# A two-layer graph attention network on one core: x moves from layer 2's residual product into its first norm, and the second norm's variance to ScalarE

## The chip, the cores and the metric

The kernel runs on one core of one Trainium2 chip. The metric is device time in microseconds from start to end of one execution; lower is better. Engines are named as in the profile: PE (TensorE, matrix products), DVE (VectorE), ACT (ScalarE), POOL (GpSimd) and SP (SyncE, which here only issues DMA transfers). Each engine works through its own instructions in the order of the program and waits where one is not yet free to run.

## The reference

Two graph attention layers (GAT) with residuals over 10,000 nodes and 170,000 edges (80,000 in each direction and 10,000 loops, and the layer adds self loops once more), then a last norm over the sum with the input:

```
def gat_conv(x, edge_index, W, a_src, a_dst, bias, heads, out_ch, concat):
    xl = (x @ W).reshape(n, heads, out_ch)
    e = leaky_relu(alpha_src[src] + alpha_dst[dst], 0.2)
    alpha = softmax of e over the edges of each dst
    out = segment_sum(xl[src] * alpha, dst)
    return out + bias

h0 = x
h = gat_conv(x, edge_index, W1, a_src1, a_dst1, b1, 4, 256, True)
h = relu(layer_norm(h, g1, be1)) + (h0 @ Wr1 + br1)
h1 = h
h = gat_conv(h, edge_index, W2, a_src2, a_dst2, b2, 1, 768, False)
h = layer_norm(h, g2, be2) + (h1 @ Wr2 + br2)
x = _layernorm(x + h)
```

x is 10,000 x 768 in fp32, h1 has 1024 columns, the output is 10,000 x 768. The last norm has no scale and no shift.

## The kernel before, in words

The 10,000 nodes are cut into 79 tiles of 128 (one node per partition). Three stages follow each other.

**Layer 0** (my name for the first loop over tiles, 0 to about 876 us): for each tile the product x W1 with its attention sums goes into a table in DRAM, one row of 1033 numbers a node. Two generators run beside it, one step a tile: `prepare` sorts the nodes by their number of edges and lists each node's neighbours ("slots"), and `weight_steps` loads W2 and Wr1 and folds vectors into them. The PSUM pool of the products has two buffers of 1024 columns.

**Layer 1** (`ordered_layer1`): the tiles are taken by degree, so that all 128 nodes of a tile have about as many neighbours: the numbers of slots n of the 79 steps rise from 8 to 41 (step 39) and fall back to 9, 1377 in all. For each slot POOL issues one indirect DMA (`gather`, L424), which brings one neighbour's table row to each of the 128 partitions. The rows land in a ring of 29 slots, in order; the gather of slot q waits until slot q - 29 is released. Of a tile's n slots the first up to four are summed on PE, by a product with a diagonal matrix of the weights that ACT builds (`summed`, L723 and L729); every fourth of the rest on DVE alone (`weigh`, L519), the others by a multiply on ACT (L508) and an add on DVE (L515). Three slots before a tile's end the logits of the next tile are made (L477 and on), which need all of its rows. At the start of step t the tile before it is normed (L572 to L800). x of the tile, itself gathered by POOL into `xt` (one buffer), is transposed by PE in `from_x` (L699), multiplied by Wr1 (L171), and written by SP to `x_d` (L707), where layer 2 finds it. The next x is gathered after seven slots of the loop and waits for that write. The tile of h1 is transposed, written to `h1_d` (L812) and multiplied by W2 (L817), which gives the rows of layer 2's table. A tile with more slots than the ring goes through `attend_parts`.

**Layer 2** (`ordered_layer2`): the same with a ring of 41 slots and rows of 770 numbers; a tile's own rows come as a plain SP transfer. Of each slot 512 columns are weighed on DVE (L519) and 256 on PE with a diagonal matrix (L927 on ACT, L928 on PE). `residual` puts x and h1 Wr2 into PSUM: x by a product with the identity (L939), then 16 blocks of h1 Wr2 (L942). `norms` runs in steps between the slots of the next tile: statistics of the weighed sum; then (after three slots) scale and shift with g2 and `be2_b`, the add of the residual (L952), and statistics of that sum; then (after six) its mean and deviation in one ACT instruction (L958); then (after nine) POOL's indirect store of the rows (L960). At the start of the layer br1 Wr2 is made by a product of its own (`q`, L965), and br2 and that row are added to `be2_b` after the first tile (L1007, L1008). `fetch_x` loads h1 and x of a tile on SP, two tiles ahead.

All of it stands in the order in which Python emits it; nothing reorders the instructions of an engine.

Of the kernel before, what the change touches and what calls it, by code (L numbers as in the profile page):

```python
# [35 lines left out]
P = 128  # L36
# [43 lines left out]
def gnn_kernel(ctx, tc, x, x_cols, src, dst, src_col, dst_col, W1, a_src1, a_dst1, b1, g1, be1, Wr1, br1,  # L80
# [56 lines left out]
    br1_c = consts.tile([P, K1], F32, name="br1_c")  # L137

# [463 lines left out]
    with tc.tile_pool(name="w1", bufs=1) as w1p, tc.tile_pool(name="l1", bufs=2) as io, \  # L602
# [75 lines left out]
    def ordered_layer1():  # L678
        nc.scalar.add_instruction(mybir.InstLoadActFuncSet(name=nc.get_next_instruction_name(), act_func_set_id=6, engine=nc.scalar.engine))
        with tc.tile_pool(name="b1", bufs=1) as pool, tc.tile_pool(name="small1", bufs=2) as small, \  # L680
# [38 lines left out]
            def summed(acc, diagonals, e, q, lo, hi, m):  # L719

                for k in range(lo, hi):
                    for i in range(H1):
                        nc.scalar.activation(diagonals[:, k * H1 + i, :], ident, AF.Copy,  # L723
                                             scale=e[:, k, i:i + 1])
                for k in range(lo, hi):
                    for i in range(H1):

                        c, d = i * DH1, (i + 1) * DH1
                        nc.tensor.matmul(acc[:, c:d], diagonals[:, k * H1 + i, :], ring.slot(q + k)[:, c:d],  # L729
                                         start=(k == 0 and c % BANK == 0),  # L730
                                         stop=(k == m - 1 and (d % BANK == 0 or d == C1)),
                                         skip_group_check=True)

            def weights_of(t):
# [6 lines left out]
                diagonals = pool.tile([P, ON_PE1 * H1, P], F32, name="diagonals")  # L741
                for lo, hi in ((0, min(m, 2)), (min(m, 2), m)):
                    summed(acc, diagonals, e, FIRST[t], lo, hi, m)
# [24 lines left out]
            for t in range(NT + 1):  # L768
# [66 lines left out]
                if live and not whole:  # L835
# [5 lines left out]
                    def some(q, e):  # L841
                        m = min(ON_PE1, e.shape[1])
                        diagonals = pool.tile([P, ON_PE1 * H1, P], F32, name="diagonals")
                        summed(sums, diagonals, e, q, 0, m, m)
# [23 lines left out]
    def ordered_layer2():  # L868
        nonlocal ps_big
        with tc.tile_pool(name="b2", bufs=1) as pool, tc.tile_pool(name="small2", bufs=2) as small, \  # L870
# [28 lines left out]
            adds = [spread(pool, shift, "out", nc.sync)]  # L899
# [3 lines left out]
            nc.vector.tensor_add(b2_b, b2_b, adds[0][:, :C2])  # L903
            adds.append(spread(pool, br2, "out", nc.sync))
# [27 lines left out]
            def residual(t):  # L932


                hT, xt = ins.pop(t)
                r = ps_big.tile([P, 2 * BANK], F32, name="big")
                for c in range(0, C2, BANK):
                    d = min(C2, c + BANK)
                    nc.tensor.matmul(r[:, c:d], ident, xt[:, c:d], start=True, stop=False,  # L939
                                     skip_group_check=True)  # L940
                    for j in range(K1):
                        nc.tensor.matmul(r[:, c:d], hT[:, j, :], wr2[:, j, c:d], start=False,  # L942
# [4 lines left out]
            def norms(t, h, r, means):  # L947
# [17 lines left out]
            q = product(brT, wr2, C2)  # L965
# [4 lines left out]
            for t in range(NT):  # L970
# [11 lines left out]
                else:  # L982
# [301 lines left out]
```

## Time and profile before

| | |
|---|---|
| median of 10 runs | 5344.74 us (5339.65 to 5348.59) |
| the profiled execution, its own time | 5345.81 us |
| its span, first to last instruction | 5343.9 us |
| mean granted PE clock | 0.946 of full speed |
| busy: PE, weight loads, DVE, ACT, POOL | 89%, 53%, 80%, 52%, 60% |
| moved by DMA | 1591.37 MB, 298 GB/s over the span |
| POOL's gathers (L424, ring) | 2675, 991 ns each |
| DVE, 512 or 256 columns of a slot (L519) | 2530, 624 ns each |
| DVE, 1024 columns of a slot (L515) | 801, 1231 ns each |
| PE, residual of layer 2 (L942) | 2464, 487 ns each |

The page gives each engine's busy time and, for the costliest groups, the idle time just before them and what ended it. Stages differ in what limits them, so the prediction reads the same figures by stretches of the span. A wait "<-issue" is time in which the profile shows nothing that was waited for. Busy times of POOL are rough, and PE's matmuls overlap, so that its share is not one of its peak.

### The profile page before, as it was taken

The numbers are of one execution on the slowest core, as the hardware profiler recorded it, in microseconds if no ns is written. First come the engines' busy times: TensorE is split into PE (matmuls) and PEld (weight loads), VectorE is DVE, ScalarE is ACT, GpSimd is POOL, SyncE is SP. The second block draws the span as 40 slices with busy tenths as digits, with TensorE's granted clock in tenths as the row PEclk, the third lists the DMA queues.
The fourth block names the chain that finished last, engine by engine and source line by source line (L and its number), as shares of the span: only waits on it lengthen the run. The fifth ranks groups of instructions, "written<-read, shape, count | busy, mean of one in ns | idle before, by whom it ended". The sixth has DMA issues, their size and how long they took to land. (4 is left out here: it accounts for less than half of the span.)

```text
span 5343.9 us, 59565 instructions
## 1 busy us (share of the span) xinstructions
PE 4768.3 (89%) x15188; PEld 2857.2 (53%) x15191; DVE 4285.0 (80%) x7729; ACT 2799.3 (52%) x8184; POOL 3231.0 (60%) x3159
## 2 busy tenths in 40 slices
PE   8999996999999986578999999999998866889998
PEld 3444443555555544345555555566666544566665
DVE  5884244899999887688899999589988767889998
ACT  3434343677778776677887777433333222223332
POOL 3446465555666654555666655277777657777774
PEclk9999998999999998789999999999998887999999
DMA  4333625899999997699999999599999989999995
GB/s 156 126 99 86 95 92 197 307 338 348 359 359 362 365 340 276 247 328 345 360 364 365 353 336 333 187 385 374 377 367 348 326 269 322 330 348 370 365 386 220
DMA packets 474306, 1591.37 MB, mean 298 GB/s; under 512 B 118327, under 2 KB 122487, under 8 KB 473958
## 3 DMA queue, kind: packets, MB, share of 16 engines
q0 software_dynamic: 322384, 1286.62, 66.0%
q1 hardware_dynamic: 149520, 297.43, 16.4%
q10 hardware_dynamic: 2054, 3.42, 0.2%
q8 instruction: 128, 2.10, 0.2%
q14 instruction: 220, 1.80, 0.1%
HBM read 1431.80 MB, written 177.29 MB: 301 GB/s over the span
## 5 line engine op out<-in xcount | busy, mean ns | idle before, releaser
L424 POOL DMA_INDIRECT ring<-table,slots x2675 | 2651.5, 991 | 1446.5 <-DVE acc L519 344.4
L519 DVE SCALAR_TENSOR_TENSOR acc<-ring,e,acc 128x512 f32<-128x512 f32 (+1 forms) x2530 | 1578.4, 624 | 127.9 <-PE acc L729 52.4
L508 ACT ACTIVATE ring<-ring,e 128x256 f32<-128x256 f32 x3284 | 1337.4, 508 | 0.0
L515 DVE TENSOR_TENSOR acc<-acc,ring 128x1024 f32<-128x1024 f32 x801 | 985.7, 1231 | 79.6 <-ACT ring L508 10.6
L928 PE MATMUL big<-ring,diagonals 128*128 128x256 f32 x2754 | 682.9, 410 | 201.0 <-ACT diagonals L927 191.2
L171 PE MATMUL big<-w,xT 128*128 128x512 f32 x1896 | 825.5, 597 | 23.3 <-DMA w<-in_W_dram 9.9
L171 PE MATMUL big<-wr,xT 128*128 128x512 f32 x1896 | 833.6, 596 | 0.2 <-ACT xT L700 0.2
L817 PE MATMUL half<-w,hT 128*128 128x512 f32 (+1 forms) x2528 | 830.4, 486 | 0.0
L942 PE MATMUL big<-wr,w 128*128 128x512 f32 (+1 forms) x2464 | 823.0, 487 | 0.0
L928 PEld LDWEIGHTS big<-ring,diagonals 128*128 128x128 f32 x2754 | 561.6, 206 | 319.3 <-ACT diagonals L927 221.1
L817 PEld LDWEIGHTS half<-w,hT 128*128 128x128 f32 x2528 | 477.8, 189 | 372.7 <-issue 310.0
L729 PE MATMUL acc<-ring,diagonals 128*128 128x256 f32 x1912 | 485.7, 412 | 203.9 <-ACT diagonals L723 203.7
L942 PEld LDWEIGHTS big<-wr,w 128*128 128x128 f32 x2464 | 469.6, 191 | 329.8 <-issue 297.9
L171 PEld LDWEIGHTS big<-w,xT 128*128 128x128 f32 x1896 | 362.0, 192 | 482.4 <-issue 464.4
L171 PEld LDWEIGHTS big<-wr,xT 128*128 128x128 f32 x1896 | 357.0, 192 | 420.5 <-issue 419.8
L729 PEld LDWEIGHTS acc<-ring,diagonals 128*128 128x128 f32 x1912 | 392.1, 208 | 289.9 <-ACT diagonals L723 226.9
L576 ACT ACTIVATE sd<-mv,eps 128x1 f32<-128x1 f32 x237 | 69.6, 294 | 813.8 <-DVE mv L574 813.7
L927 ACT ACTIVATE diagonals<-ident,e 128x128 f32<-128x128 f32 x1377 | 411.2, 387 | 141.1 <-DVE e L499 121.3
L723 ACT ACTIVATE diagonals<-ident,e 128x128 f32<-128x128 f32 x956 | 292.8, 387 | 204.3 <-DVE e L499 204.0
L660 DVE TENSOR_TENSOR scr<-big,ad_b 128x1024 f32<-128x1024 f32 x79 | 96.7, 1224 | 376.4 <-ACT row L657 376.4
L485 ACT ACTIVATE e<-e 128x68 f32<-128x68 f32 (+29 forms) x160 | 38.2, 239 | 650.7 <-DVE e L484 650.7
L665 POOL TENSOR_TENSOR row<-row,none 128x1024 f32<-128x1024 f32 x79 | 187.1, 2369 | 261.8 <-ACT row L657 260.7
(172 smaller groups left out, 3618.1 us busy)
## 6 DMA issues: line engine op xcount, KB each, us to landing
ring<-table,slots POOLq DMA_INDIRECT x2675, 6.9
table<-row SPq DMA_DIRECT2D x79, 516.0 KB, 3.5
h_d<-hT SPq DMA_DIRECT2D x79, 512.0 KB, 6.9
w<-h_d SPq DMA_DIRECT2D x77, 512.0 KB, 8.3
table<-row SPq DMA_DIRECT2D x79, 385.0 KB, 6.9
ring<-table SPq DMA_DIRECT2D x79, 385.0 KB, 6.5
xT<-in_x_cols_dram SPq DMA_DIRECT2D x79, 384.0 KB, 4.4
x_d<-xt SPq DMA_DIRECT2D x79, 384.0 KB, 7.2
```

Source lines behind the costliest of these rows:

```text
L171: nc.tensor.matmul(p[:, c:e], aT[:, j, :], w[:, j, c:e], start=(j == 0), stop=(j == k - 1))
L424: nc.gpsimd.indirect_dma_start(out=to, out_offset=None, in_=table, in_offset=bass.IndirectOffsetOnAxis(ap=index, axis=0), **more)
L508: nc.scalar.activation(row[:, s], row[:, s], AF.Copy, scale=e[:, h:h + 1])
L515: nc.vector.tensor_add(acc[:, :c], acc[:, :c], row[:, :c])
L519: nc.vector.scalar_tensor_tensor(acc[:, s], row[:, s], e[:, h:h + 1], (acc if first is None else first)[:, s], op0=OP.mult, op1=OP.add)
L665: nc.gpsimd.tensor_add(row[:, :C1], row[:, :C1], b1_b)
L723: nc.scalar.activation(diagonals[:, k * H1 + i, :], ident, AF.Copy, scale=e[:, k, i:i + 1])
L729: nc.tensor.matmul(acc[:, c:d], diagonals[:, k * H1 + i, :], ring.slot(q + k)[:, c:d], start=(k == 0 and c % BANK == 0), stop=(k == m - 1 ...
L817: nc.tensor.matmul(q, hT[:, j, :], w2[:, j, c:c + q.shape[1]], start=(j == 0), stop=(j == K1 - 1))
L927: nc.scalar.activation(diagonals[:, k % G, :], ident, AF.Copy, scale=e[:, k, :])
L928: nc.tensor.matmul(to, diagonals[:, k % G, :], ring.slot(FIRST[t] + k)[:, ON_PE2:C2], start=False, stop=(k == n - 1), skip_group_check=True)
L942: nc.tensor.matmul(r[:, c:d], hT[:, j, :], wr2[:, j, c:d], start=False, stop=(j == K1 - 1 and (d < C2 or not whole(t))), skip_group_check= ...
```

## The change

- A constant tile `after2` (128 x 768) is made in layer 0: be2 + br2 + br1 Wr2, spread over the partitions. Eight more steps of `weight_steps` each load one block of 128 rows of Wr2 on SP, multiply it by a block of br1 on PE, and add the result to `after2` on DVE.
- In layer 1 POOL adds `after2` to `xt` in place, after the transposes and before SP writes it to `x_d`.
- The diagonal matrices of layer 1 are in three buffers of one slot each in place of one buffer of four slots, and each slot's matrices are built and used in turn.
- In layer 2 `residual` no longer has x in it. x comes into three buffers in turn (one of them `after2`'s, free by then), and stands where `be2_b` stood, as the added vector of the first norm. be2, br2 and the product br1 Wr2 are gone from the start of the layer.
- The add of the residual is one DVE instruction that also sums its rows (`accum_out`). From the sum ACT makes the mean, the variance by a square with an accumulator, the deviation, and the normed rows. The statistics of the second norm on DVE are gone.

```diff
@@ constants
+    after2 = consts.tile([P, C2], F32, name="after2")
@@ weight_steps
             load(w2, W2)
+            nc.sync.dma_start(after2, bass.AP(tensor=be2.tensor, offset=be2.offset, ap=[[0, P], [1, C2]]))
+            part = spread(w1p, br2, "part", nc.sync)
...
             load(wr1, Wr1)
+            nc.vector.tensor_add(after2, after2, part)
+            for k in range(K1):
+                part = w1p.tile([P, C2], F32, name="part")
+                nc.sync.dma_start(part, Wr2[k * P:(k + 1) * P, :])
+                yield
+                q = product(brT[:, k:k + 1, :], part[:, None, :], C2)
+                nc.vector.tensor_add(after2, after2, q[:, :C2])
             yield
@@ layer 1, from_x
                 moves = halves(xT, xt)
+                nc.gpsimd.tensor_add(xt, xt, after2)
                 nc.sync.dma_start(x_d[t], xt)
@@ layer 1, summed
-            def summed(acc, diagonals, e, q, lo, hi, m):
+            def summed(acc, e, q, lo, hi, m):
                 for k in range(lo, hi):
+                    diagonals = pool.tile([P, H1, P], F32, name="diagonals", bufs=3)
                     for i in range(H1):
-                        nc.scalar.activation(diagonals[:, k * H1 + i, :], ident, AF.Copy,
-                                             scale=e[:, k, i:i + 1])
-                for k in range(lo, hi):
+                        nc.scalar.activation(diagonals[:, i, :], ident, AF.Copy, scale=e[:, k, i:i + 1])
                     for i in range(H1):
                         c, d = i * DH1, (i + 1) * DH1
-                        nc.tensor.matmul(acc[:, c:d], diagonals[:, k * H1 + i, :], ring.slot(q + k)[:, c:d],
+                        nc.tensor.matmul(acc[:, c:d], diagonals[:, i, :], ring.slot(q + k)[:, c:d],
@@ layer 2, start
-            brT = at_end(C1).rearrange("p (k n) -> p k n", n=P)
-            nc.vector.tensor_copy(brT, br1_c[:, :, None].to_broadcast([P, K1, P]))
-            firsts = [(at_end(C1), at_end(D0)) for _ in range(min(2, NT))][::-1]
+            firsts = [at_end(C1) for _ in range(min(2, NT))][::-1]
+            xs = [parts[2][:, :D0], parts[3][:, :D0], after2]
             def fetch_x(t):
-                hT, xt = firsts[t] if t < 2 else (parts[t % 2], parts[2 + t % 2][:, :D0])
+                hT = firsts[t] if t < 2 else parts[t % 2]
                 nc.sync.dma_start(hT, h1_d[t])
-                nc.sync.dma_start(xt, x_d[t])
-                return hT.rearrange("p (k n) -> p k n", n=P), xt
+                nc.sync.dma_start(xs[t % 3], x_d[t])
+                return hT.rearrange("p (k n) -> p k n", n=P)
...
-            g2_b, be2_b = (spread(pool, v, n, nc.sync) for v, n in ((g2, "g2"), (be2, "be2")))
-            adds.append(spread(pool, br2, "out", nc.sync))
+            g2_b = spread(pool, g2, "g2", nc.sync)
@@ layer 2, residual
-                    nc.tensor.matmul(r[:, c:d], ident, xt[:, c:d], start=True, stop=False,
-                                     skip_group_check=True)
                     for j in range(K1):
-                        nc.tensor.matmul(r[:, c:d], hT[:, j, :], wr2[:, j, c:d], start=False,
+                        nc.tensor.matmul(r[:, c:d], hT[:, j, :], wr2[:, j, c:d], start=(j == 0),
@@ layer 2, norms
-                scaled(h, means, stats, g2_b, be2_b)
-                nc.vector.tensor_add(h, h, r[:, :C2])
-                mean, inv = deviation(small, pieces(h, C2 // 2))
+                scaled(h, means, stats, g2_b, xs[t % 3])
+                total = small.tile([P, 1], F32, name="all")
+                nc.vector.scalar_tensor_tensor(h, r[:, :C2], 1.0, h, op0=OP.mult, op1=OP.add, accum_out=total)
                 yield
+                o = pool.tile([P, C2], F32, name="out")
                 less = small.tile([P, 1], F32, name="less")
-                nc.vector.scalar_tensor_tensor(less, mean, -1.0, inv, op0=OP.mult, op1=OP.mult)
-                o = pool.tile([P, C2], F32, name="out")
-                nc.scalar.activation(o, h, AF.Identity, bias=less, scale=inv)
+                nc.scalar.activation(less, total, AF.Copy, scale=-1.0 / C2)
+                nc.scalar.activation(o, h, AF.Square, bias=less, accum_out=total)
+                nc.scalar.activation(total, total, AF.Ln, bias=eps, scale=1.0 / C2)
+                nc.scalar.activation(total, total, AF.Exp, scale=-0.5)
+                nc.scalar.activation(less, less, AF.Copy, scale=total)
+                nc.scalar.activation(o, h, AF.Identity, bias=less, scale=total)
@@ layer 2, before and in the loop
-            q = product(brT, wr2, C2)
...
-                    if not t:
-                        nc.vector.tensor_add(be2_b, be2_b, adds[1])
-                        nc.vector.tensor_add(be2_b, be2_b, q[:, :C2])
```

More of the change, by code (lines that the diff above doesn't have):

```diff
@@ L740, in weights_of @@
                 acc = ps_acc.tile([P, 2 * BANK], F32, name="acc")
-                diagonals = pool.tile([P, ON_PE1 * H1, P], F32, name="diagonals")
                 for lo, hi in ((0, min(m, 2)), (min(m, 2), m)):
-                    summed(acc, diagonals, e, FIRST[t], lo, hi, m)
+                    summed(acc, e, FIRST[t], lo, hi, m)
                     yield acc
@@ L842, in some @@
                         m = min(ON_PE1, e.shape[1])
-                        diagonals = pool.tile([P, ON_PE1 * H1, P], F32, name="diagonals")
-                        summed(sums, diagonals, e, q, 0, m, m)
+                        summed(sums, e, q, 0, m, m)
                         return sums, m
@@ L884, in at_end @@
                 return flat[:, rest:rest + n]
-            brT = at_end(C1).rearrange("p (k n) -> p k n", n=P)
-            nc.vector.tensor_copy(brT, br1_c[:, :, None].to_broadcast([P, K1, P]))
-            firsts = [(at_end(C1), at_end(D0)) for _ in range(min(2, NT))][::-1]
+            firsts = [at_end(C1) for _ in range(min(2, NT))][::-1]
+            xs = [parts[2][:, :D0], parts[3][:, :D0], after2]
             def fetch_x(t):
-                hT, xt = firsts[t] if t < 2 else (parts[t % 2], parts[2 + t % 2][:, :D0])
+                hT = firsts[t] if t < 2 else parts[t % 2]
                 nc.sync.dma_start(hT, h1_d[t])
-                nc.sync.dma_start(xt, x_d[t])
-                return hT.rearrange("p (k n) -> p k n", n=P), xt
+                nc.sync.dma_start(xs[t % 3], x_d[t])
+                return hT.rearrange("p (k n) -> p k n", n=P)
             ins = {0: fetch_x(0)}
             ring.fetch(SLOTS[0])
-            adds = [spread(pool, shift, "out", nc.sync)]
+            added = spread(pool, shift, "out", nc.sync)
             b2_b = spread(pool, b2, "b2", nc.sync)
             ins[1] = fetch_x(1)
-            g2_b, be2_b = (spread(pool, v, n, nc.sync) for v, n in ((g2, "g2"), (be2, "be2")))
-            nc.vector.tensor_add(b2_b, b2_b, adds[0][:, :C2])
-            adds.append(spread(pool, br2, "out", nc.sync))
+            g2_b = spread(pool, g2, "g2", nc.sync)
+            nc.vector.tensor_add(b2_b, b2_b, added[:, :C2])
             assert SLOTS[0] <= rest // R2 and NT > 1
@@ L932, in residual @@
             def residual(t):
-                hT, xt = ins.pop(t)
+                hT = ins.pop(t)
                 r = ps_big.tile([P, 2 * BANK], F32, name="big")
```

## The prediction

> **What bounds the kernel now.** I read the busy times by stage first, because the whole-span shares mix three stages. Columns: stretch in us, its length, busy us of PE, PE's weight loads, DVE, ACT and POOL with instruction counts, granted clock, DMA share, GB/s. The cuts are mine: layer 1 runs from 876 to 3443 us, layer 2 after it.
>
> ```profile
> 876.00:1480.00 604.00, 545.14 (x1785) 318.31 (x1786) 519.30 (x871) 415.07 (x1105) 354.61 (x349) 0.96 0.92 339
> 1480.00:1830.00 350.00, 329.43 (x1113) 199.89 (x1113) 316.77 (x508) 279.03 (x754) 224.67 (x218) 0.99 0.98 363
> 1830.00:2510.00 680.00, 502.38 (x1620) 313.89 (x1620) 550.84 (x876) 477.84 (x1280) 385.78 (x382) 0.86 0.85 308
> ...
> 3496.00:4064.00 568.00, 550.00 (x1944) 372.10 (x1944) 517.67 (x1056) 193.85 (x612) 429.74 (x445) 0.97 0.99 373
> 4064.00:4780.00 716.00, 544.54 (x1850) 381.79 (x1850) 532.75 (x1002) 198.44 (x636) 484.12 (x505) 0.85 0.90 319
> 4780.00:5270.00 490.00, 468.97 (x1665) 316.54 (x1664) 455.62 (x925) 165.27 (x523) 371.75 (x384) 0.98 0.99 374
> ```
>
> PE, DVE and the DMA engines all stand above 0.9 outside the middle, so no one share names the bound. The timeline of POOL does, for layer 2 (start, duration, line; idle time before it in brackets):
>
> ```profile
> 3759.33 0.95 POOL L424 DMA_INDIRECT ring<-table,slots  x1 [0.30 <-PE big L942]
> 3760.59 0.95 POOL L424 DMA_INDIRECT ring<-table,slots  x1 [0.30 <-issue]
> 3761.85 1.01 POOL L960 DMA_INDIRECT out_dram<-out,order  x1 [0.31 <-issue]
> 3763.16 0.98 POOL L424 DMA_INDIRECT ring<-table,slots  x1 [0.30 <-issue]
> ```
>
> A gather costs POOL 0.96 + 0.30 us, back to back. From 3496 to 4064 it issues 445 of them, 568/445 = 1.276 us each; from 4780 to 5270 384, again 1.276. POOL never rests in these stretches, whoever is named as releaser: they are POOL's (and at share 0.99 the DMA engines'), and a cheaper DVE or PE leaves them as they are. From 4064 to 4780 505 issues would need 505 x 1.276 = 644 of 716 us: 72 us of slack is all that can be won there.
>
> In layer 1 POOL has slack, but its place in the order matters. First POOL, then PE, where tile 45 (22 slots) begins:
>
> ```profile
> 2426.84 0.99 POOL L424 DMA_INDIRECT ring<-table,slots  x1 [0.75 <-issue]
> 2428.13 1.00 POOL L424 DMA_INDIRECT ring<-table,slots  x1 [0.30 <-PE acc L729]
> 2430.23 1.08 POOL L424 DMA_INDIRECT ring<-table,slots  x1 [1.09 <-PE acc L729]
> 2431.96 0.99 POOL L424 DMA_INDIRECT ring<-table,slots  x1 [0.65 <-PE acc L729]
> 2433.70 0.99 POOL L424 DMA_INDIRECT ring<-table,slots  x1 [0.74 <-PE half L699]
> 2435.80 0.99 POOL L424 DMA_INDIRECT ring<-table,slots  x1 [1.11 <-DVE acc L519]
> ...
> 2440.94 0.97 POOL L424 DMA_INDIRECT xt<-in_x_dram,order  x1 [1.47 <-PE big L171]
> 2442.21 0.99 POOL L424 DMA_INDIRECT ring<-table,slots  x1 [0.30 <-issue]
> ```
>
> ```profile
> 2423.40 10.03 PE L729 MATMUL acc<-ring,diagonals 128*128 128x256 f32 x32 [4.75 <-ACT diagonals L723]
> 2433.26 0.82 PE L699 MATMUL half<-ident,xt 128*128 128x128 f32 x6
> ```
>
> 2426.84 is the last gather of the tile before, 2428.13 to 2433.70 refill slots 0 to 3, freed one by one by PE's diagonals, and PE transposes x only after them.
>
> **Layer 0: +27 us.** Eight weight steps get a K=1-row product (`product` on one row block: two fp32 passes each of 512 and 256 columns), a 384 KB load on SP and a DVE add. On PE 0.87 + 0.43 = 1.3 us (the starts of L939 and of L942 after it, same shapes); on DVE 0.953 (L952), which fits: a tile comes every 10.3 us and DVE has 9.0 in the busiest (two multiplies 2.45, three L239 passes 5.3, their follow-ups 1.3). The product takes the second of two PSUM buffers, so the next tile's product needs the buffer of the tile just finished: ACT's copy (1.0, L657) and two multiplies (2 x 1.22, L660), 3.4 us in which PE now runs on in the other buffer. 8 x 3.4 = 27; bounds 8 x 1.3 = 10 and, with a late load, 35. PE is the bound here (843 of 876 us), so it counts.
>
> **Layer 1: +80 us.** POOL gets one 128x768 add a tile: 187.1/79 = 2.37 us for 1024 columns (L665), so 1.78. Its wait is the larger thing. It stands behind the last gather of the tile before and ahead of slot 0's, and it overwrites `xt`, so it waits for the transposes. In tile 45: add 2434.2 to 2436.0, slot 0 at 2436.3 instead of 2428.1, then 1.3 us each, slot 4 at 2441.5 instead of 2435.8. SP's `x_d` store follows the add and takes 7.2 us, but the x gather has moved as far. I went through POOL's rows of all tiles this way, keeping every release where it is: slot 0 comes 2.3 to 4.3 us late in tiles of up to 15 slots, 5 to 9 in the larger; POOL has caught up to within 2 us at each tile's end, so nothing accumulates by itself.
>
> Who waits for a late gather: the logits of the next tile (L477), three slots before this tile's end. With a ring of 29, the last gather that they need follows the release of slot n(t)+n(t+1)-30. Two stretches of DVE's waits:
>
> ```profile
> DVE e L477 <- DMA ring<-table,slots: 1.3, 3, 0.6
> ...
> DVE e L477 <- DMA ring<-table,slots: 17.0, 5, 4.5
> ```
>
> The first is 1480 to 1830, the second 1760 to 2110 us. By the landings that the trace gives, the last gather is in 6 to 28 us early for n up to 16, 1 to 9 for 17 and 18, and 0 to 2 for 19 and more. So: (a) n up to 16 nothing: PE, 552 of 583 us busy from 2860 to 3443, hides it; 17 and 18, 17 tiles, a delay of 4 to 6 against that slack and DMA engines at 0.98 that lose their queue: 0.5 each, 8. (b) n = 19 to 21, 17 tiles: 3 to 5 late, of which an emptier queue gives back 2 (issue to landing 5.9 us at the median, 3.5 at the fifth percentile): 2 each, 34. (c) n of 22 and more, 11 tiles: 2.2 to 5.4 late, DMA share already 0.83 to 0.92 and landings 3.4 to 4.7 after issue, nothing given back: 3.5 each, 38. Sum 80, and 2 at the first tile, where the x store waits behind 29 gathers. Bounds: 10 (if the queue hides all but 1 us in (c)) and 200 (2.5, 4.5 and 5.5 us, with (a) on 25 tiles). No row has the add beside layer 1's work; I stay below the middle because a queue smooths.
>
> The three diagonal buffers cost nothing: the fourth build waits for the first slot's matmuls, and PE waits for ACT here (4.75 above), not ACT for PE. If PE were late, ACT would stand for one slot's eight passes, 1.8 us, with its multiplies behind it.
>
> The Trainium skill, "SBUF — State Buffer", section "Who interferes with whom", speaks against the add beyond this: a VectorE instruction with two SBUF inputs and a GpSimd one that reads SBUF exclude each other for a whole instruction. L588 (1.28 us, h and be1 both in SBUF) stands near the add; by the rule up to 1.8 x 79 = 142 us more would be DVE's, an estimate; no row of before has such a pair.
>
> **Layer 2: -24 us.** Per tile DVE loses the add (0.953), two statistics (1.02 together), the aggregate (0.209) and L956 (0.153), 2.33, and gets one pass of 0.95 to 1.02 plus an accumulator read (0.08, L239's): -1.25, 99 us in all. PE loses 1.3 a tile, 103 in all. ACT gains a square (1.02 as L958) and two small ones (0.2): 1.4 a tile on an engine at 0.3; no table load is added in the program. In POOL's stretches none of it shows. In 4064 to 4780 DVE waits 73.7 us for gathers in the rising half alone, and the removed work lies after the release that the awaited gather follows (third slot and `turn`) unless n is 23 or more: 8 tiles x 1.25 = 10. At the start the 16-matmul product goes, but DVE waits for gathers (6.67 at 3465): 3. POOL's small rests at n = 14 and below: 5. After the last gather (5275) DVE is the bound: 4.5 tiles x 1.25 = 6. Bounds -5 and -60 (most of the 72, and these). The x load now waits for L588 of three tiles earlier, and x is wanted only in the norm, three tiles after its load: free. If it were late, DVE would stand in L588.
>
> **Sum.** +27 + 82 - 24 = +85 on the profiled execution's 5345.81 (span 5343.9; median of the runs 5344.74, 0.02% off): 5430.
>
> **Rivals.** *Gathers land in time.* The ring and the DMA queue take up POOL's detour. For it: POOL catches up in each tile; against: (c)'s landings with no slack. Then 10 + 10 - 55 = -35, 5310. It decides if the late slot costs under 1 us a tile and the middle of layer 2 gives back most of its 72. *DMA engines starve every tile.* Between the last gather and slot 0 there are now 6 to 10 us against 1.3, more than a landing. For it: share 0.98 in 1480 to 1830; against: 0.92 before that. +35 + 190 - 5, 5565. *Only the largest tiles suffer*, (c) alone with half the price in layer 0: 14 + 40 - 24 = +30, 5375. That the change does not do what it says: the add and the pass stand in the built order, so only that DVE's saving is visible, -99: a part of the first rival.
>
> **Numbers.** Forecast 0.50 (own range 5395 to 5480), only the largest 0.20, starving 0.10, in time 0.20. The runs tell 0.2% (11 us) from nothing. Faster 0.18, same 0.07, slower 0.75; 5320 to 5510 leaves out half of the first rival and most of the starving.
>
> **What would show it.** Right: in 1830 to 2510 POOL's L424 after the new add, DVE's L477 waits up by tens of us, layer 1 longer, layer 2's POOL stretches unchanged at 1.276 us. Wrong: L477's wait unchanged, or issues in layer 2 still back to back but fewer us in 3496 to 4064, or a new wait of DVE on POOL.

## The result and the profile after

The changed kernel takes 5504.03 us (median of 8 runs, 5498.52 to 5513.34) against 5346.24 us for the kernel before (28 runs beside it). The ratio is 1.0298, 95% interval 1.0289 to 1.0307: about 158 us slower. The profiled execution took 5507.73 us, its span 5505.9.

I cut both spans at the DVE instruction that applies a tile's deviation and shift in its norm (L588 before, L589 after), for the first and the last tile of each layer:

| stretch | before, us | after, us | difference | forecast |
|---|---|---|---|---|
| start to layer 1's first norm (layer 0 and one tile) | 926.4 | 977.1 | +50.6 | +29 |
| layer 1, first to last norm | 2493.8 | 2623.0 | +129.1 | +80 |
| to layer 2's first norm | 74.5 | 71.4 | -3.1 | -3 |
| layer 2, first to last norm | 1831.8 | 1817.1 | -14.7 | -21 |
| rest | 17.3 | 17.3 | 0.0 | 0 |

The differences add up to +162, the two spans' own difference. By stretches (columns as in the prediction; the first three lie in layer 1, the others in layer 2):

```profile
927.00:1530.00 603.00, 543.85 (x1783) 317.49 (x1784) 518.46 (x870) 415.20 (x1105) 384.31 (x369) 0.96 0.90 338
1530.00:1900.00 370.00, 327.78 (x1073) 199.73 (x1074) 303.18 (x481) 270.75 (x728) 224.80 (x218) 0.94 0.86 325
1900.00:2660.00 760.00, 517.76 (x1661) 325.30 (x1660) 565.40 (x904) 487.31 (x1307) 422.91 (x407) 0.83 0.76 284
3671.00:4240.00 569.00, 520.71 (x1840) 355.14 (x1839) 484.91 (x975) 231.46 (x724) 431.41 (x447) 0.96 0.99 373
4240.00:4950.00 710.00, 515.55 (x1759) 365.27 (x1758) 505.16 (x935) 231.36 (x724) 482.18 (x506) 0.84 0.91 322
4950.00:5440.00 490.00, 450.82 (x1578) 306.12 (x1577) 431.07 (x866) 197.80 (x621) 370.84 (x386) 0.96 0.99 376
```

In the second line the DMA share is 0.86 where it was 0.98, in the third 0.76 where it was 0.85, with every engine lower too: something holds up all of them. In layer 2 POOL still issues back to back (569/447 = 1.273 us, 490/386 = 1.269), while PE, at 0.92 of the fourth line, was at 0.97.

The page's groups of the new instruction and of the store behind it (for the first, after the bar: busy us and mean ns, then the idle time before it and what ended it; the second is an issue, with its KB and its time to landing):

```profile
L717 POOL TENSOR_TENSOR xt<-xt,after 128x768 f32<-128x768 f32 x79 | 145.2, 1838 | 408.5 <-PE half L709 408.5
x_d<-xt SPq DMA_DIRECT2D x79, 384.0 KB, 2.3
```

The add itself is 145 us of an engine with slack; the 408.5 us that POOL stood still for PE's transposes are the news. In the timeline, POOL where a tile of 19 slots begins, and DVE near its end (start, duration, line; idle time before it in brackets):

```profile
1724.62 0.98 POOL L425 DMA_INDIRECT ring<-table,slots  x1 [1.77 <-ACT diagonals L735]
1725.91 0.99 POOL L425 DMA_INDIRECT ring<-table,slots  x1 [0.30 <-issue]
1734.02 1.82 POOL L717 TENSOR_TENSOR xt<-xt,after 128x768 f32<-128x768 f32 x1 [7.12 <-PE half L709]
1735.99 1.00 POOL L425 DMA_INDIRECT ring<-table,slots  x1
...
1751.53 0.23 DVE L478 TENSOR_TENSOR e<-ring 128x44 f32<-128x44 f32 x1
1756.07 0.19 DVE L478 TENSOR_TENSOR e<-ring 128x32 f32<-128x32 f32 x1 [4.30 <-DMA ring<-table,slots]
```

Gathers stop at 1726.9 and go on at 1736.0, nine microseconds later: PE frees slots 0 to 3 in that time, one by one, but their gathers stand behind the add, which waits for the transposes that PE does last. At 1751.8 DVE has the first 11 slots' logits of the next tile and stands 4.3 us for the rows of the rest. In the middle of the layer that wait stood as follows (view of waits; total us, times, longest): before, from 1960 to 2610 us

```profile
DVE e L477 <- DMA ring<-table,slots: 32.2, 11, 6.5
```

and after, from 2010 to 2660 us, the same tiles:

```profile
DVE e L478 <- DMA ring<-table,slots: 81.0, 15, 9.9
```

Layer 0, PE's waits from 200 to 480 us after the change:

```profile
PE big L172 <- issue: 18.5, 8, 2.4
PE big L172 <- DMA part<-in_Wr_dram: 16.6, 1, 16.6
```

Seven stalls of 2.3 us, one behind each weight step but the first (the eighth in the line, of 2.4 us, stands before the change too), and at the first step one stall of 16.6 us that the prediction does not have.

### The profile page after: what moved, and what is told of

Same layout as the page of the kernel before. It is cut to its first block, busy times and chain, and to the rows that moved or that the text cites. A ratio compares the mean times of both kernels' runs of the same rounds, so it can differ in the third digit from the quotient of the medians.

```text
span 5505.9 us, 58830 instructions
## 1 busy us (share of the span) xinstructions
PE 4710.8 (86%) x14872; PEld 2828.3 (51%) x14875; DVE 4193.7 (76%) x7498; ACT 2909.9 (53%) x8500; POOL 3341.3 (61%) x3238
## 5 line engine op out<-in xcount | busy, mean ns | idle before, releaser
L425 POOL DMA_INDIRECT ring<-table,slots x2675 | 2616.7, 978 | 1128.0 <-issue 339.9
L934 PE MATMUL big<-ring,diagonals 128*128 128x256 f32 x2754 | 699.8, 418 | 284.8 <-ACT diagonals L933 255.0
L946 PE MATMUL big<-wr,w 128*128 128x512 f32 (+1 forms) x2464 | 808.8, 486 | 4.9 <-DMA w<-h_d 4.9
L934 PEld LDWEIGHTS big<-ring,diagonals 128*128 128x128 f32 x2754 | 574.0, 211 | 408.8 <-ACT diagonals L933 312.1
L739 PE MATMUL acc<-ring,diagonals 128*128 128x256 f32 x1912 | 508.2, 427 | 313.2 <-ACT diagonals L735 313.1
L739 PEld LDWEIGHTS acc<-ring,diagonals 128*128 128x128 f32 x1912 | 410.3, 217 | 403.7 <-ACT diagonals L735 333.9
L717 POOL TENSOR_TENSOR xt<-xt,after 128x768 f32<-128x768 f32 x79 | 145.2, 1838 | 408.5 <-PE half L709 408.5
```

The costliest lines, as they stand in the source:

```text
L425: nc.gpsimd.indirect_dma_start(out=to, out_offset=None, in_=table, in_offset=bass.IndirectOffsetOnAxis(ap=index, axis=0), **more)
L739: nc.tensor.matmul(acc[:, c:d], diagonals[:, i, :], ring.slot(q + k)[:, c:d], start=(k == 0 and c % BANK == 0), stop=(k == m - 1 and (d % ...
L934: nc.tensor.matmul(to, diagonals[:, k % G, :], ring.slot(FIRST[t] + k)[:, ON_PE2:C2], start=False, stop=(k == n - 1), skip_group_check=True)
```

## The experiments

### Layer 1: the wait or the work?

The new add can cost by its 1.8 us of work, by the wait for PE's transposes in front of it, or by what the two do together. Four kernels take one of these away. They ran once each, at a time when layer 2 took 2039 to 2051 us in all four, some 220 us longer than in the profile above (the kernel before took 5630.12 us beside them, one run); why is not known. So they are compared by layer 1's stretch alone, first to last norm.

**No add.** The line goes; the three diagonal buffers and all of the rest stay.

```diff
-                nc.gpsimd.tensor_add(xt, xt, after2)
```

> The changed kernel without POOL's add of after2 to xt: x goes to x_d as it was gathered, so be2 + br2 + br1 Wr2 is left out of the output. Everything else stays, the three diagonal buffers too. Layer 1, from its first to its last norm, took 2493.8 us before and 2623.0 changed. If the add and its place in POOL's queue are the cause, it goes back to 2490 to 2500, and the whole to about 5375. If the three diagonal buffers (or the later use of x) are the cause, it stays at 2600 or more and the whole near 5500.

Measured: 5621.81 us; layer 1 in 2498.6 us, where the kernel before has 2493.8 and the changed one 2623.0. The add is 124 of the 129 us that layer 1 lost.

**The wait without the work.** One column is added, so the instruction waits as before but does next to nothing.

```diff
-                nc.gpsimd.tensor_add(xt, xt, after2)
+                nc.gpsimd.tensor_add(xt[:, :1], xt[:, :1], after2[:, :1])
```

> POOL's add at the same place on one column of xt alone (the other 767 columns of the vector are left out of x): the wait for the transposes stays, the 1.8 us of work go down to about 0.1 to 0.2. If the wait in the queue is the cause, layer 1 keeps most of its 129 us: the slot 0 gather was held 7 us by the wait and 1.8 by the work, so 85 to 105 of 129. If the work on POOL (or its reads of SBUF against DVE's) is the cause, it loses most of it: under 40 left.

Measured: 5739.64 us; layer 1 in 2601.3, that is 102.7 more than without the add. Its group, from 930 to 3600 us:

```profile
L717 POOL TENSOR_TENSOR xt<-xt,after 128x1 f32<-128x1 f32 x79 | 17.1, 216 | 403.6 <-PE half L709 403.6
```

216 ns of work, and the same 404 us of standing still.

**The work without the wait.** An add of the same size at the same place, on a tile that nobody else touches.

```diff
-                nc.gpsimd.tensor_add(xt, xt, after2)
+                nc.gpsimd.tensor_add(after2, after2, after2)
```

> POOL's add at the same place and of the same size, on after2 and itself, so that nothing waits for PE; x goes to x_d as gathered, and the vector is left out. The work stays, the wait goes. Queue theory: 1.8 us in a queue that waited for slots to be freed there anyway, 0 to 25 us in layer 1. Rival (the work, or the SBUF port shared with DVE): 80 us or more stay. Sum check: with the run on one column it should make about 129.

Measured: 5650.23 us; layer 1 in 2519.1, 20.5 more than without the add. Wait and work by themselves make 102.7 + 20.5 = 123.2, together (in the profile above) 2623.0 - 2498.6 = 124.4: they simply add. This add reads one operand twice and took 1.47 us, not 1.84, so the work's part is a little low.

**Wait and work, at another place.** The add and the store come after the gathers that refill the slots summed on PE.

```diff
-                nc.gpsimd.tensor_add(xt, xt, after2)
-                nc.sync.dma_start(x_d[t], xt)
+                def put(t=t, xt=xt):
+                    nc.gpsimd.tensor_add(xt, xt, after2)
+                    nc.sync.dma_start(x_d[t], xt)
+
+                puts.append(put)
...
+                if live:
+                    events.insert(0, (first - 1, puts.pop()))
```

> The whole add with its wait, but placed in POOL's queue (and the store of x in SP's) after the gathers of the slots that PE sums, in place of ahead of slot 0's. By then the transposes are done and POOL would wait for slot 4 anyway. Queue theory: layer 1 within 0 to 40 us of before's 2493.8. Rival (any add between gathers costs its time, or x's later store holds up the next x gather): 80 us or more stay.

Measured: 5644.40 us; layer 1 in 2523.2, 24.6 more than without the add. From 930 to 3600 us:

```profile
L719 POOL TENSOR_TENSOR xt<-xt,after 128x768 f32<-128x768 f32 x79 | 144.3, 1827 | 39.4 <-PE half L709 37.7
L425 POOL DMA_INDIRECT xt<-in_x_dram,order x79 | 77.0, 974 | 175.4 <-DMA x_d<-xt 151.9 <-issue 12.7 <-DMA table<-row 6.2
```

The same add, but POOL now stands 39 us for the transposes and not 409. It stands 152 us before the x gather, which waits for the later store (91 us in the kernel before, 6.5 with the add at its first place); by then the slots' gathers are out, and layer 1 is 100 us shorter than with the add at its first place. So a hundred of the 124 us are the place of one waiting instruction in POOL's order.

### Layer 1: the three diagonal buffers

The kernel before with that part of the change alone (diff as in the change, function `summed`).

> The kernel before with one part of the change alone: layer 1's diagonal matrices in three buffers of one slot in place of one of four. Mine: nothing, layer 1 (first to last norm) 2485 to 2505 us and the whole within 10 us of before on the same chip. Rival (ACT's fourth build waits for PE and holds its multiplies): up to 1.8 us a tile, 60 to 140 us more.

Measured: 5345.96 us beside 5342.9 (median of 15 runs, 5337.41 to 5348.63); layer 1 in 2497.4, against 2493.8. They cost nothing that can be seen. Layer 2 of this kernel is that of the kernel before, and here it took 1825.4 us instead of 1831.8, 5.8 of the difference in steps 25 to 50, its middle. So a difference of 6 us in layer 2 between two single traces, most of all one in the middle, says nothing by itself.

### Layer 0: the eight weight steps

The changed kernel, with Wr1's 3 MB loaded after the eight blocks and the products in the small PSUM buffers, a bank at a time, so that no buffer of the tiles' products is taken.

```diff
-            load(wr1, Wr1)
...
-                q = product(brT[:, k:k + 1, :], part[:, None, :], C2)
-                nc.vector.tensor_add(after2, after2, q[:, :C2])
+                for c in range(0, C2, BANK):
+                    d = min(C2, c + BANK)
+                    q = ps_tr.tile([P, BANK // P, P], F32, name="tr").rearrange("p a b -> p (a b)")
+                    nc.tensor.matmul(q[:, :d - c], brT[:, k, :], part[:, c:d], start=True, stop=True)
+                    nc.vector.tensor_add(after2[:, c:d], after2[:, c:d], q[:, :d - c])
+            load(wr1, Wr1)
```

> The changed kernel with two edits in layer 0 alone: Wr1 is loaded after the eight loads of Wr2's blocks and not ahead of them, and the eight products go into the small PSUM buffers that prepare uses, one bank at a time, so that they do not take a buffer of the tiles' products. Layer 0 up to layer 1's first norm took 926 us before and 977 changed. If the 16.6 us stall is the 3 MB load in front and the 2.3 us stalls are the PSUM buffer, PE's stalls there go and layer 0 loses 30 to 40 of the 51 us. If the stalls are the loads of the blocks themselves, or DVE, it loses under 15.

Measured: 5479.21 us; layer 1's first norm at 948.3 us, against 977.1 after the change and 926.4 before. That is 28.8 back of 50.6, a little under the 30 to 40 that I expected. The 2.3 us stalls at the steps are gone, so the PSUM buffer was their cause; the long one is still most of its size (PE's waits, 200 to 480 us):

```profile
PE tr L655 <- DMA part<-in_Wr_dram: 11.7, 1, 11.7
```

So the long load of Wr1 in front of it was the smaller part of those 16.6 us. The timeline of the changed kernel has the larger:

```profile
239.90 0.43 SPq L592 DMA_DIRECT2D wr<-in_Wr_dram  x1
...
244.37 0.95 DVE L648 TENSOR_TENSOR after<-after,part 128x768 f32<-128x768 f32 x1
...
245.35 0.33 SPq L651 DMA_DIRECT2D part<-in_Wr_dram  x1
...
253.09 2.90 PE L172 MATMUL big<-part,brT 128*128 128x512 f32 x4 [16.64 <-DMA part<-in_Wr_dram]
```

The block goes into the one `part` buffer, which still holds br2. SP can issue its load only when DVE has added br2 (244.37 to 245.32), and DVE comes to that after the sorting passes of `prepare`; the load is out 0.03 us later and lands 7.7 us after that, while PE, in order, stands in front of the block's product.

### Layer 2: who is the bound?

**Without POOL's scatter.** The changed kernel, with the rows stored by SP in the order in which they are made.

```diff
-                nc.gpsimd.indirect_dma_start(
-                    out=out, out_offset=bass.IndirectOffsetOnAxis(ap=nodes(t), axis=0),
-                    in_=o, in_offset=None, bounds_check=N - 1, oob_is_err=False)
+                u = TURNS[t] * P
+                nc.sync.dma_start(out[u:min(u + P, N), :], o[:min(u + P, N) - u])
```

> The changed kernel with layer 2's result stored by SP as plain rows in the order of the node numbers of the tile's place, not scattered by POOL: the reordering of the output is left out, the bytes are the same. POOL loses 79 issues of 1.3 us, 103 us. If POOL's issue is what sets layer 2 outside its middle, some 54 tiles get 1.3 us shorter: layer 2 is 50 to 80 us shorter than in the run with the two edits in layer 0 on the same chip. If the DMA engines (share 0.99) set it, it stays within 15 us.

Measured: 5412.42 us; layer 2 in 1732.8 us, against 1817.0 in the run before this one, whose layer 2 is the changed kernel's. Windows inside POOL's first back-to-back stretch, first this kernel, then that of the layer 0 experiment:

```profile
3733.00:4200.00 467.00, 442.10 (x1583) 303.04 (x1582) 415.67 (x829) 197.86 (x619) 347.68 (x364) 0.97 1.01 391
```

```profile
3710.00:4210.00 500.00, 463.42 (x1635) 317.78 (x1634) 428.58 (x857) 203.71 (x640) 379.40 (x394) 0.96 0.99 373
```

POOL still issues almost without a pause, 467/364 = 1.283 us each, but all of these are gathers now, and the DMA engines moved 391 GB/s at a share of 1.01 where they moved 373 at 0.99. A share of 0.99 was not yet their limit: POOL's issue was the bound, and 79 issues fewer are worth 79 x 1.28 = 101 us at most, 84 by measurement. A gather's own time on POOL is the same in both windows, 0.96 us.

**The constant row by PE.** Here the change's layer 2 is kept, but nothing is added in layers 0 and 1: the row be2 + br2 + br1 Wr2 goes into PSUM by an fp32 product with a row of ones.

```diff
+                    nc.tensor.matmul(r[:, c:d], ones, row[:, c:d], start=False,
+                                     stop=(d < C2 or not whole(t)), skip_group_check=True)
```

> A version without POOL's add and without the steps in layer 0: layers 0 and 1 as before; in layer 2 x is the first norm's added vector and the variance is on ACT as in the change, and be2 + br2 + br1 Wr2 comes into the residual by a product of ones with one row. PE keeps 1.3 us a tile there, DVE saves 1.25. From the parts (start -3, layer 2 -15 in the changed kernel): 10 to 20 us faster than before, 0.2 to 0.4%. If PE's saving was what gave the 15 us, nothing is left: within 5 us.

Measured: 5350.57 us, ratio 1.0014 (1.0005 to 1.0023): slower than before (5342.9), where 10 to 20 us less was expected. Layer 2 took 1848.0 us, 16 more than before; its trace is of the slowest of eleven executions (5358.33), so 16 is on the high side.

**The constant row by DVE.** The same, with one DVE add a tile in place of that product.

```diff
+                nc.vector.tensor_add(xs[t % 3], xs[t % 3], be2_b)
                 scaled(h, means, stats, g2_b, xs[t % 3])
```

> As in the run with the row on PE, nothing is added in layers 0 and 1; but the constant row is added to x by one more DVE instruction a tile in layer 2 (128x768 from SBUF, about 0.95 us), so that PE keeps the saving of the identity products (about 1.3 us a tile) while DVE's saving falls from 1.25 to about 0.3 us a tile. Mine (PE's saving is what made layer 2 shorter): layer 2 from first to last norm 1815 to 1822 us against before's 1831.8, total 5 to 14 us under before. Rival (DVE's saving made it shorter): layer 2 within 4 us of before, total within 6 us of it. Second rival (ACT's longer chain of small steps at the layer's end eats the gain): the last tile 14 us or more as in the run with the row on PE, total 0 to 8 us under before.

Measured: 5349.51 us beside 5342.78, ratio 1.0011 (1.0002 to 1.0020), layer 2 in 1838.3 us, 6.5 more than before. A miss for all three theories: PE kept its saving, DVE was no heavier, the last tile took 10.0 us (not 14.7), and still the layer did not get shorter. Windows from 3560 to 4060 us of the kernel before, of the row on PE, and of the row on DVE:

```profile
3560.00:4060.00 500.00, 486.66 (x1732) 331.17 (x1731) 455.87 (x927) 171.29 (x542) 378.28 (x392) 0.98 0.99 372
```

```profile
3560.00:4060.00 500.00, 491.66 (x1722) 321.59 (x1720) 417.08 (x834) 196.46 (x613) 373.81 (x385) 0.99 0.98 366
```

```profile
3560.00:4060.00 500.00, 452.82 (x1598) 309.04 (x1598) 441.64 (x868) 200.86 (x629) 381.50 (x387) 0.96 0.98 367
```

With the row on PE, that engine is at 491.7 of 500 us: a second bound, and heavier than before, since the one-row product costs more than the identity's. With the row on DVE, PE is at 452.8 and DVE at 441.6, and yet POOL gets out 387 issues and not 392. Its own time says why. POOL's gathers in this window, before and with the row on DVE (after the bar: busy us, mean ns):

```profile
L424 POOL DMA_INDIRECT ring<-table,slots x367 | 352.9, 962 | 114.4 <-issue 30.4 <-PE big L928 23.5 <-DVE acc L519 15.4
```

```profile
L424 POOL DMA_INDIRECT ring<-table,slots x363 | 358.1, 986 | 111.3 <-PE big L930 25.3 <-issue 24.0 <-DVE acc L519 15.8
```

A gather became 24 ns longer in the mean. The timeline of the row on DVE shows which ones:

```profile
3613.96 0.95 DVE L951 TENSOR_TENSOR w<-w,be 128x768 f32<-128x768 f32 x1
3614.28 1.48 POOL L424 DMA_INDIRECT ring<-table,slots  x1 [0.30 <-DVE acc L519]
...
3632.66 0.98 POOL L424 DMA_INDIRECT ring<-table,slots  x1 [0.30 <-DMA ring<-table,slots]
3633.83 1.02 DVE L588 SCALAR_TENSOR_TENSOR w<-w,sd,x 128x768 f32<-128x768 f32 x1
3633.94 1.72 POOL L424 DMA_INDIRECT ring<-table,slots  x1 [0.30 <-PE big L930]
3635.97 0.95 POOL L424 DMA_INDIRECT ring<-table,slots  x1 [0.31 <-DVE w L954]
```

A gather that starts while DVE runs an instruction with both inputs in SBUF (the new L951, or L588) can take up to 1.7 us instead of 0.95. In this window 31 gathers start so, 1.321 us in the mean (18 of them took 1.27 to 1.73, the others 0.94 to 0.98), and 331 do not, 0.955. Before, 21 start during L588, 1.089 in the mean (5 of them took 1.30 to 1.67), and 345 do not, 0.954. When the gather starts decides: in the kernel before, from 3500 us on, 15 gathers start within the first 0.1 us of an L588 and take 0.95 to 0.98 us; 31 start 0.1 to 0.9 us into one, and every one of them ends 0.82 to 0.85 us after L588 does, whenever it began. So, by these times, a gather has a step early in it that stands until DVE's instruction ends. Above 0.949 us that is 11.5 us lost in 500, against 2.9 (L588, at its new place in time, holds up 11 of the 18). Layer 2 has about 1,060 us in which POOL is back to back, so by this estimate the second such add a tile costs (11.5 - 2.9) x 1060/500 = 18 us.

**The constant row by PE, in bf16.** Neither a one-row fp32 product nor an add on DVE: the row is cut into three bf16 rows whose sum it is, and one product with 65 rows (three of them used) puts it into PSUM. The first two tiles take it by a DVE add.

```diff
+                    if t >= 2:
+                        nc.tensor.matmul(r[:, c:d], ones3, row3[:, c:d], start=False,
+                                         stop=(d < C2 or not whole(t)), skip_group_check=True)
```

> As in the run with the row on PE, x is the first norm's vector, the second variance is ACT's, and layers 0 and 1 are those of before; but the constant row goes into PSUM as three bf16 rows in one product with 65 rows, and not as one fp32 row, so that PE keeps most of the identity's 1.3 us a tile and DVE all of its 1.25 us, and no second DVE add with both inputs in SBUF is there. Mine (layer 2 gets shorter where PE's and DVE's savings both stay and POOL's gathers aren't lengthened): gathers of the first 500 of layer 2 at 0.96 to 0.97 us as before, layer 2 from first to last norm 1812 to 1822 us against 1831.8, total 8 to 18 us under before. Rival (the layer is POOL's, and the change's 15 us came from its shorter start): layer 2 within 5 us of before's, total within 6 us of it.

Measured: 5342.22 us against 5351.54 of the kernel before (21 runs beside it), ratio 0.9982 (0.9973 to 0.9991): faster than before, by 9 us or 0.2%, and the best version of all. Layer 2 took 1819.5 us, 12.3 less than before and 18.8 less than with the row on DVE, close to the 18 us just worked out. By the medians, each beside its own runs of the kernel before, the two are 16 us apart (9.3 under, 6.7 over). Its window from 3560 to 4060 us, with 393 issues of POOL and PE at 470:

```profile
3560.00:4060.00 500.00, 470.35 (x1683) 322.06 (x1682) 427.36 (x855) 204.53 (x643) 379.41 (x393) 0.96 0.99 373
```

**One pass for scale and residual.** The last step along this line: x stays in PSUM as before; from the third tile on the constant row joins it in bf16, and DVE scales and adds the residual in one instruction, which reads one input from PSUM. There L588 is gone.

```diff
+                    nc.vector.scalar_tensor_tensor(h, h, stats[1], r[:, :C2], op0=OP.mult, op1=OP.add,
+                                                   accum_out=total)
```

> Before, with the constant row in PSUM as three bf16 rows, x still there by its identity product, and the first norm's scale and the add of the residual in one DVE instruction (h times the reciprocal deviation plus PSUM, with row sums); the second variance is ACT's. A tile loses L588 (1.02 us, the only DVE instruction of it with both inputs in SBUF), L952 becomes a pass of about 0.96, the statistics go: about 2.3 us of DVE; PE gets some 0.4 us. Mine (a gather that starts while L588 runs takes 1.6 us and not 0.95, so POOL gains about 0.2 us a tile, and DVE's end gains 2.3 us on each of the last tiles): mean gather of POOL's back-to-back stretches 0.955 to 0.962 us, total 8 to 25 us under before. Rival (PE is the bound there, 487 of 500 us busy, and is 0.4 us a tile heavier): layer 2 longer than before as in the run with the row on PE, total 5 to 20 us over. Second rival (DVE's time counts for nothing but at the end): 5 to 10 us under.

Measured: 5347.00 us beside 5351.54, ratio 0.9989 (0.9980 to 0.9998), 4.5 us under before, where I expected 8 to 25; layer 2 in 1826.0 us (cut at L586, since L588 is gone), 5.8 less than before, no more than one kernel's own two traces differ. Its window and its gathers from 3560 to 4060 us:

```profile
3560.00:4060.00 500.00, 489.02 (x1775) 330.33 (x1774) 401.48 (x827) 205.96 (x640) 372.70 (x390) 0.99 0.99 371
```

```profile
L424 POOL DMA_INDIRECT ring<-table,slots x366 | 349.0, 953 | 120.0 <-PE big L934 33.4 <-issue 32.7 <-DMA ring<-table,slots 13.1
```

Gathers are the shortest of all runs, 953 ns (0.955 to 0.962 us expected), but PE is back at 489 of 500 us, and the second line puts more of POOL's idle time down to it than before (33.4 us). DVE lost the most here (401 us against 456), and the layer gained less than with the row in bf16 and x on DVE.

## Why the prediction was right, and where it was off

The forecast, +85 us with the time inside 5395 to 5480, names the right sign in all three places and, for layer 1, the right mechanism. The size is off: 158 us were measured, nearly twice as much. The measured 5504.03 lies above the likeliest case's own range, and within the wide one (5320 to 5510) by only 6 us, which is luck.

**Layer 1.** By the length of each step against the same step before: up to step 20 (17 slots and fewer) the two kernels are 0.2 us apart, and from step 54 to the layer's end 1.0, so "(a) n up to 16 nothing" holds. Seventeen and 18 slots (15 tiles, where the prediction counts 17) lost about 10 us together, where it has 8; nearly all of it with 18. Term (c), 22 slots and more, lost 46 us over 12 tiles, 3.9 each, where it has 3.5. What failed is the size of term (b), 19 to 21 slots: "3 to 5 late, of which an emptier queue gives back 2 ... 2 each, 34". These 17 tiles lost 75 us, 4.4 each: 41 of the 49 us that the forecast of this layer is short. The queue was emptier, as the DMA engines' share of 0.86 instead of 0.98 and the landing of the x store in 2.3 us instead of 7.2 suggest, but nothing that it gave back can be seen: DVE's waits for rows rose, and POOL's gathers landed no sooner. Their times to landing, where the trace gives them (1480 to 1830 us before, then 1530 to 1900 after):

```profile
DMA to landing us min/median/max: 5.0/7.1/10.8
```

```profile
DMA to landing us min/median/max: 4.3/7.4/8.9
```

The late slots cost about what they were late. The rival "the queue takes up the detour" fell with it, and so did "starving every tile", as tiles of up to 17 slots lost nothing.

That it is mostly the wait and its place, less the add's work, was the prediction's reading, and the runs show it: 102.7 us for the wait, 20.5 for the work, 24.6 for both at a later place.

**Layer 0.** The step of 3.4 us is about right: 1.3 us of product, eight times, and a stall of 2.3, seven times, make 26.5 us of the 27. What is missing is mostly a wait that the prediction left out. It costed a "late load" only as an upper bound of 35 in all, and did not ask what the first load waits for: the `part` buffer, which DVE frees late. That is 16.6 us. Another 5 us are three tile products of 12.2 us instead of 10.5 right after such stalls (see the last section).

**Layer 2.** -17.8 with the start, against -24. The start gave 3.1, as priced, and POOL's stretches are unchanged, as the prediction said. Steps 5 to 11 were 1.25 us shorter each, DVE's whole saving, but then POOL was the bound and by step 24 only 0.5 us was left of it. The middle (steps 25 to 50) gave 5.1 where 10 was forecast, but the unchanged layer 2 of the run with the diagonal buffers alone differs by 5.8 there, so whether the middle gave anything stays open. Steps 51 to 74 gave 5.2 for the 5 of "POOL's small rests", and the last three tiles 1.3 each, the price of the prediction, 3.9 of its 6.

**The port.** The prediction cites the Trainium skill, "SBUF — State Buffer", section "Who interferes with whom": a VectorE instruction with two SBUF inputs and a GpSimd one that reads SBUF keep each other out for a whole instruction. It says that no row of before has such a pair. That was wrong: the gathers, whose index columns `slots` lie in SBUF, behave like such instructions, and the trace of before has them (timeline, layer 2):

```profile
3765.70 0.95 POOL L424 DMA_INDIRECT ring<-table,slots  x1 [0.30 <-DVE acc L519]
...
3766.79 1.02 DVE L588 SCALAR_TENSOR_TENSOR w<-w,sd,be 128x768 f32<-128x768 f32 x1
3766.96 1.67 POOL L424 DMA_INDIRECT ring<-table,slots  x1 [0.30 <-issue]
```

For the new add the rule shows, but seldom, since the two rarely meet. An L589 was running at the start of six of the 79 adds; four of these took 2.15 to 2.51 us, while L589 kept its 1.28. Here it is POOL that stands (timeline after the change):

```profile
1272.23 1.28 DVE L589 SCALAR_TENSOR_TENSOR h<-h,sd,be 128x1024 f32<-128x1024 f32 x1 [0.46 <-DVE h L587]
1272.68 2.51 POOL L717 TENSOR_TENSOR xt<-xt,after 128x768 f32<-128x768 f32 x1 [2.60 <-PE half L709]
```

That is 2.51 us instead of the median 1.81. In the run with the work alone, it was DVE that stood: two L589 that began 0.24 and 0.97 us into POOL's add took 2.33 and 1.60 us. Over all 79 adds the mean is 1.838, so about (1.838 - 1.813) x 79 = 2 us, not the 142 of the estimate from the rule, in which every add met one. The same page says that a DMA which seems stalled by a VectorE instruction is one whose descriptors GpSimd writes, and that GpSimd was kept from its port; the run with the row on DVE fits that, with 1.32 us in the mean for a gather that starts during such an instruction and 0.955 for one that doesn't. But the same section has a probe in which a `tensor_tensor` did not stall a DMA, and here 7 of the 15 gathers that started during the TENSOR_TENSOR L951 took 1.44 to 1.73 us: the measurement decides. That the port is the cause is the page's reading: the runs show the wait for DVE's end and its price, not the port.

## What to carry over

On an engine that issues gathers in order, look first at where an instruction that waits is put, then at how long it works: here the wait cost five times the work, and moving it behind the next four gathers took back 100 of 124 us. Where an engine's issue is the bound, work taken from others is worth something only in its rests, at the layer's end, or where it shortens the issue itself; so here a saving of about 100 us by sum on each of DVE and PE was worth 15 in layer 2. And count a freed buffer's last reader before a load is called early.

## What the hardware showed that was not expected

- A DMA share of 0.99 was no limit: with fewer scatters the same engines moved 391 GB/s instead of 373.
- A gather's issue is lengthened by DVE instructions with both inputs in SBUF, 1.32 us in the mean against 0.955: begun 0.1 to 0.9 us into an L588 of the kernel before, it ended 0.82 to 0.85 us after it. It goes away with them: with L588 gone, and an instruction with one input in SBUF and one in PSUM in its place, the mean of all gathers was 0.953.
- A product of one fp32 row with ones took more of PE than that of 128 rows with the identity: 1.59 us a tile by the starts of the instructions against 1.29, and PE's busy time in the 500 us shown went from 486.7 to 491.7. The reason stays open.
- In layer 0 three products of a tile took 12.2 us instead of 10.5 after PE had stood. The granted clock accounts for it: it was 0.86 in these and 1.00 in the others, and 10.5/0.86 = 12.2. Two of them (columns as in the prediction; the clock is the third number from the end):

```profile
270.90:283.10 12.20, 12.20 (x25) 5.35 (x26) 6.95 (x10) 2.10 (x12) 2.94 (x3) 0.86 0.37 124
286.70:297.20 10.50, 10.49 (x25) 4.76 (x26) 6.96 (x10) 2.12 (x12) 2.94 (x3) 1.00 0.45 144
```

Right after the stall of 16.6 us it was 0.50, and a block's product took 2.90 us instead of 1.45. Both tile products shown come after a stall of 2.29 us; why only some of them get a lower clock is not shown.
